# Layer-1 experts of a fused two-layer kernel: the 176 inner rows as 128 and 48 instead of 88 and 88

## The chip, the core and the metric

The kernel runs on one core of one Trainium2 chip. The metric is the device time of one execution in microseconds (us). Before the change the median of three runs is 1293.78 us (1292.96 to 1298.01). One further execution was recorded by the hardware profiler; all views quoted here come from it.

## The reference, cut to what matters

Two transformer layers on x of shape 2 x 1024 x 128 in fp32. The change lies in the second layer's mixture of experts. There are 2048 tokens, 16 experts, and each token goes to four of them:

```python
g = jnp.einsum('th,eih->tei', x, gate_proj)      # gate_proj, up_proj: 16 x 176 x 128
u = jnp.einsum('th,eih->tei', x, up_proj)
act = jax.nn.silu(g) * u
y = jnp.einsum('tei,ehi,te->th', act, down_proj, combine_w)   # down_proj: 16 x 128 x 176
```

`combine_w` is zero except for the four experts a token has chosen. So 8192 pairs of token and expert have to go through a 128 -> 176 -> 128 gated product.

## The kernel before

**Slots and blocks.** The tokens are sorted by expert. Each expert gets a whole number of blocks of 128 slots; at most 79 blocks are needed (`NBLK`), and 79 are always computed. `sort1` computes on VectorE the slot of every choice (`slot_of`, L861) and the weight row of every block (`weight_row`). `scatter` (L898, GpSimd) writes token rows of 512 bytes to `slots_x` in DRAM; `gather` (L910) later reads rows of 512 bytes from `slots_y` in DRAM, multiplied by their share and added to the residual on GpSimd.

**Weights.** `regroup` (L884 to L890) copies, early in the kernel, the weights of every expert into one DRAM table `wx`: for each expert 128 rows of `WX` = 608 floats (2432 bytes), namely 176 gate columns, 176 up columns and two lots of 128 down columns. The inner 176 rows are handled as two halves of 88 (`I1H`), so only 88 of the 128 rows of the down part are used and the other 40 are filled with zeros.

**The stage of the experts.** It is one stretch of the second layer's attention: the loop at the end of the kernel writes the order of TensorE by hand, and at step `EXPERTS` = 67 of 129 it calls `experts()`, which issues all 79 blocks with no attention work between them. All other engines get their order from the scheduler; each engine, and the queue of SP that issues nearly all DMAs, runs its instructions strictly in that order.

For each block i:

- `fetch_w(i)` (SP, L948) brings the 128 x 608 weights of the block's expert into a ring of 6 places. Four places are the tiles that held the normalised tokens and their transposes; two are in the tiles `p` of the attention ("room" in the trace). Blocks 0 to 3 are fetched before the stage, at step `EXPERTS - 2`.
- `fetch_x(g)` (SP, L959) brings four blocks of tokens; `turn_x(g)` transposes them (TensorE L974, ScalarE L976).
- `hidden(i)`: four products on TensorE with weights of 128 rows x 88 columns (L984), sigmoid on ScalarE (L987), two multiplications on VectorE (L988, L989), each on 88 partitions x 256.
- `outputs(i)`, two blocks later: two products with a contraction of 88 (L999) accumulate into one 128 x 128 result. Every four blocks ScalarE copies the results (L1002) and SP stores them to `slots_y` (L1003).

The slots of a group of four blocks lie in DRAM as "(i p) d": row 128 i + p of the group is partition p of block i, so a transfer of a group moves pieces of 512 bytes.

**Tiles that the change shares.** `by_position` writes its result `rel` (L1139, L1141) in the pool `early`, of which there is one buffer, and sends it to DRAM (`bounce`, L1148); `near_by` reads it back skewed (`near`, L1159). Steps 65 and 70 call them for the group of queries that the attention scans next.

An fp32 product counts as two MATMUL instructions in the trace (a transposition as one), so a block has 8 of L984 and 4 of L999.

Of the kernel before, what the change touches and what calls it, by code (L numbers as in the profile page):

```python
# [10 lines left out]
F32 = mybir.dt.float32  # L11
# [7 lines left out]
P = 128  # L19
D = 128  # L20
# [13 lines left out]
E1, I1, K1, G1, KG1 = 16, 176, 4, 4, 2  # L34
M0 = E0 * I0 // P
SH1 = 2 * I1
I1H = I1 // 2
WX = 4 * I1H + 2 * D

NBLK = (B * T * K1 + E1 * (P - 1)) // P  # L40
NTT = B * NT
# [8 lines left out]
def fused_layers_kernel(ctx: ExitStack, tc: tile.TileContext, a: dict, out: bass.AP):  # L50
# [348 lines left out]
                nc.scalar.copy(yT, y)  # L399


    slots_x = dram.tile([NBLK * P, D], F32, tag="slots_x", name="slots_x")
    wx = dram.tile([E1 * P, WX], F32, tag="wx", name="wx")
    slots_y = dram.tile([NBLK * P, D], F32, tag="slots_y", name="slots_y")

# [416 lines left out]
    def sort1():  # L822

        wide = [P, NTT, E1]
        some = l1w.tile(wide, F32, tag="some", name="some")
        at = l1w.tile(wide, F32, tag="at", name="at1")
        count = l1w.tile([P, 4, E1], F32, tag="count", name="count")
        n_tok, n_blk, start_, end_ = (count[:, i, :] for i in range(4))
        slot = l1w.tile([P, NTT, K1], F32, tag="slot", name="slot")
        flat = [t.rearrange("p t e -> p (t e)") for t in (some, at)]  # L830
        nc.vector.tensor_add(some, chosen[0], chosen[1])
        nc.vector.tensor_add(some, some, chosen[2])
        yield
# [12 lines left out]
        nc.vector.tensor_add(at[:, 1:, :], at[:, 1:, :], some[:, 0:NTT - 1, :])  # L846
        by_e = [P, E1, E1]
        nc.vector.tensor_tensor(some, spread(n_tok, NTT), filled.unsqueeze(1).to_broadcast(by_e), ALU.is_gt)
        nc.vector.tensor_reduce(n_blk, some, AX.X, ALU.add)
        yield  # L850
        nc.vector.tensor_tensor(some, lower, n_blk.unsqueeze(1).to_broadcast(by_e), ALU.mult)
        nc.vector.tensor_reduce(start_, some, AX.X, ALU.add)
        nc.vector.tensor_add(end_, start_, n_blk)
        nc.vector.tensor_scalar(start_, start_, float(P), None, ALU.mult)
        yield
        nc.vector.tensor_tensor(at, at, start_.unsqueeze(1).to_broadcast(wide), ALU.add)
        for j in range(K1):
            nc.vector.tensor_mul(some, chosen[j], at)
            nc.vector.tensor_reduce(slot[:, :, j], some, AX.X, ALU.add)
            yield  # L860
        nc.vector.tensor_copy(slot_of, slot)  # L861
        row = l1w.tile([P, NBLK], F32, tag="row", name="row")
        for lo in range(0, NBLK, NTT):
            n = min(NTT, NBLK - lo)
            nos = block_no[:, lo:lo + n]
            nc.vector.tensor_tensor(some[:, 0:n, :], end_.unsqueeze(1).to_broadcast([P, n, E1]),
                                    spread(nos, E1), ALU.is_le)
            nc.vector.tensor_reduce(row[:, lo:lo + n], some[:, 0:n, :], AX.X, ALU.add)
            yield
        nc.vector.tensor_scalar(row, row, float(E1 - 1), float(P), ALU.min, ALU.mult)  # L870
        nc.vector.tensor_copy(weight_row, row[0:1, :])

    def clear(i):

        n = min(4, NBLK - 4 * i)
        nc.sync.dma_start(slots_x[4 * i * P:(4 * i + n) * P, :].rearrange("(i p) d -> p i d", p=P),
                          zeros.unsqueeze(1).to_broadcast([P, n, D]))

    def regroup(i):


        by_row = wx.rearrange("(e p) w -> p e w", p=P)
        if i < 2:
            nc.sync.dma_start(by_row[:, :, i * I1:(i + 1) * I1],  # L884
                              a[("gproj", "uproj")[i]].rearrange("p (e w) -> p e w", e=E1))
        else:
            c = slice(2 * I1 + (i - 2) * D, 2 * I1 + (i - 1) * D)
            nc.sync.dma_start(wx.rearrange("(e p) w -> e p w", p=P)[:, 0:I1H, c],
                              a["dproj"].rearrange("(e j p) d -> j e p d", j=2, p=I1H)[i - 2])
            nc.sync.dma_start(by_row[I1H:P, :, c], zeros[I1H:P].unsqueeze(1).to_broadcast([P - I1H, E1, D]))  # L890

    scatters, fetched = [], {}

# [36 lines left out]

    held = {}
    block_w, block_x, block_xT, block_h, block_y, first_row = {}, {}, {}, {}, {}, {}

    def fetch_w(i):
        if i >= NBLK:
            return
        if i % 6 < 4:
            t = const.tile([P, T], F32, tag=("xn10", "xn11", "xT10", "xT11")[i % 6], name="blockw")
        else:
            t = held["p"][i % 2][:, 0:T]  # L940
# [7 lines left out]
        nc.sync.dma_start(t[:, 0:WX], wx[bass.ds(first_row.pop(i), P), :])  # L948
        block_w[i] = t

    def fetch_x(g):
        if 4 * g >= NBLK:
            return
        n = min(4, NBLK - 4 * g)
# [4 lines left out]
        d = nc.sync.dma_start(  # L959
            t[:, 0:n, :], slots_x[4 * g * P:(4 * g + n) * P, :].rearrange("(i p) d -> p i d", p=P)  # L960
        )
# [5 lines left out]
    def turn_x(g):  # L967
        if 4 * g >= NBLK:
            return
        n = min(4, NBLK - 4 * g)  # L970
        ps = quads(small())
        x = block_x.pop(g)
        for i in range(n):
            nc.tensor.transpose(ps[:, i, :], x[:, i, :], ident)  # L974
        t = quads(held["p"][1][:, T + TB * (g % 2):T + TB * (g % 2 + 1)])
        nc.scalar.copy(t[:, 0:n, :], ps[:, 0:n, :])  # L976
        block_xT[g] = t

    def hidden(i):

        w, xT = block_w[i], block_xT[i // 4][:, i % 4, :]
        ps = quads(small())[0:I1H]
        for j in range(4):
            nc.tensor.matmul(ps[:, j, :], w[:, j * I1H:(j + 1) * I1H], xT, start=True, stop=True)  # L984
        sg = w[0:I1H, WX:WX + 2 * P].rearrange("p (i c) -> p i c", c=P)
        h = pools["late"].tile([P, 2, P], F32, tag="bh", name="bh", bufs=3)[0:I1H]
        nc.scalar.activation(sg, ps[:, 0:2, :], AF.Sigmoid)  # L987
        nc.vector.tensor_mul(sg, ps[:, 0:2, :], sg)  # L988
        nc.vector.tensor_mul(h, ps[:, 2:4, :], sg)  # L989
        block_h[i] = h  # L990

    def outputs(i):
        g, n = i // 4, min(4, NBLK - i // 4 * 4)
        if i % 4 == 0:
            block_y[g] = quads(small())
        ps, h, w = block_y[g], block_h.pop(i), block_w.pop(i)
        for j in range(2):
            c = 4 * I1H + j * D
            nc.tensor.matmul(ps[:, i % 4, :], h[:, j, :], w[0:I1H, c:c + D], start=(j == 0), stop=(j == 1))  # L999
        if i % 4 == n - 1:  # L1000
            t = quads(pools["late"].tile([P, TB], F32, tag="yu", name="by"))
            nc.scalar.copy(t[:, 0:n, :], ps[:, 0:n, :])  # L1002
            nc.sync.dma_start(  # L1003
                slots_y[4 * g * P:(4 * g + n) * P, :].rearrange("(i p) d -> p i d", p=P), t[:, 0:n, :]
            )

    def experts():

        held["p"] = [pools["late"].tile([P, NG * TB], F32, tag="p", name="room", bufs=2) for _ in range(2)]
        turn_x(0)  # L1010
        for i in range(4, 6):
            fetch_w(i)
        for i in range(NBLK + 2):
            if i < NBLK:
                hidden(i)
            if i >= 2:
                outputs(i - 2)
                fetch_w(i + 4)
            if i % 4 == 1:
                turn_x(i // 4 + 1)  # L1020
                fetch_x(i // 4 + 2)

    yT1 = {}

# [582 lines left out]
```

## Time and profile before

| what | value |
|---|---|
| median of three runs | 1293.78 us |
| the profiled execution | 1295.13 us, of which 1293.0 us from first to last instruction |
| mean granted TensorE clock | 0.956 |
| TensorE matmul busy | 1161.0 us, 90% |
| VectorE, ScalarE, GpSimd busy | 782.9, 613.0, 370.4 us |
| DMA | 204.77 MB, mean 158 GB/s |
| the stage of the experts, from its first product to the first product of the attention behind it | 868.77 to 995.17 us |

The page cuts the span in 40 slices of 32.3 us; the stage fills the end of the 27th, the next three and most of the 31st:

```profile
PE   5989899989989777897999999988999999998997
PEclk8999999998999867899999999999999999998998
DMA  6955843445233331363356645579996454563511
```

Each digit is a share in tenths. In the stage both TensorE and the DMA engines are at 9, and nowhere else are the DMA engines that busy for so long.

Transfers of the stage, as the page lists them (size, count):

```profile
blockw<-wx SPq DMA_DIRECT2D x53, 304.0 KB
room<-wx SPq DMA_DIRECT2D x26, 304.0 KB
```

To read the other views: a line of a timeline has the start, the time to the last end, engine, line of the code, operation, output and inputs, shape and count; on TensorE "128\*88" stands for weights of 128 rows and 88 columns. PE are the products, PEld the loads of their weights. "[3.77 <-DMA room<-wx]" is idle time before the line and what ended it. In the chain of waits each line is the work, wait or transfer that the end of the kernel depended on at that time.

### The profile page before, as it was taken

What the parts mean: (1) busy time and instruction counts of PE and PEld (TensorE: products, weight loads), DVE (VectorE), ACT (ScalarE), POOL (GpSimd) and SP (SyncE); (2) the same over time, 40 slices, a digit from 0 to 9 for tenths busy, and PEclk for the clock granted to TensorE, in tenths of its full rate; (3) what the DMA queues carried; (4) which work ended last, traced back from release to release, by engine and by line L of the source; (5) the groups of instructions that cost most, each with busy time, mean ns of one, the idle gap of its engine ahead of it and who ended that gap; (6) DMA issues with size and microseconds to landing.
All of it is one profiled execution on the core that took longest, in us unless ns stands there. A gap on an engine that the chain in (4) does not pass through costs nothing.

```text
span 1293.0 us, 24010 instructions
## 1 busy us (share of the span) xinstructions
PE 1161.0 (90%) x8781; PEld 577.1 (45%) x8781; DVE 782.9 (61%) x2420; ACT 613.0 (47%) x1102; POOL 370.4 (29%) x475
## 2 busy tenths in 40 slices
PE   5989899989989777897999999988999999998997
PEld 2233232354533233443444344458998444443434
DVE  7565654376434756877866756764555766665653
ACT  3644444545655211453555645453444545554463
POOL 1223155310044610001003444320000445445454
PEclk8999999998999867899999999999999999998998
DMA  6955843445233331363356645579996454563511
GB/s 186 238 152 156 259 126 110 133 128 149 85 93 122 111 106 49 98 196 99 125 170 211 208 138 169 188 229 281 288 287 201 138 185 158 174 216 120 174 50 29
DMA packets 196313, 204.77 MB, mean 158 GB/s; under 512 B 26436, under 2 KB 178244, under 8 KB 196196
## 3 DMA queue, kind: packets, MB, share of 16 engines
q1 hardware_dynamic: 189892, 190.12, 47.7%
q0 software_dynamic: 6304, 13.12, 3.4%
q8 instruction: 70, 1.15, 0.4%
q14 instruction: 47, 0.39, 0.1%
HBM read 121.29 MB, written 90.42 MB: 164 GB/s over the span
## 4 chain that ended last, share of the span: by engine, by line
PE 63%; DVE 19%; DMA 8%; issue 5%; ACT 3%; POOL 2%; SPq 0%; POOLq 0%; DVEq 0%; ACTq 0%
PE sm L1245 11%; PE sm L1184 8%; PE acc L1264 8%; PE sm L1235 5%; PE big L731 4%; PE acc L758 4%; PE sm L984 4%; DVE maxima L1209 3%; PE big L362 3%; DVE junk L1204 3%; PE sm L1135 3%; PE big L363 2%; DMA got<-slots_y,slot_of 2%; PE ffn L391 2%; DMA room<-wx 2%
## 5 line engine op out<-in xcount | busy, mean ns | idle before, releaser
L1252 ACT ACTIVATE p<-sm 128x512 f32<-128x512 f32 x512 | 264.8, 605 | 231.3 <-PE sm L1245 224.2
L1209 DVE TENSOR_REDUCE maxima<-sm 128x1 f32<-128x512 f32 (+3 forms) x472 | 226.8, 502 | 101.6 <-PE sm L1184 101.6
L737 ACT ACTIVATE at<-big 128x1024 f32<-128x1024 f32 (+1 forms) x192 | 144.9, 809 | 139.4 <-PE big L731 134.1
L1204 DVE CUSTOM_DVE_ANT_0 junk<-sm,near 128x384 f32<-128x384 f32 (+2 forms) x292 | 130.3, 446 | 64.3 <-PE sm L1184 63.9
L1264 PE MATMUL acc<-p,vs 128*32 128x512 f32 (+1 forms) x1288 | 145.2, 520 | 0.4 <-issue 0.4
L1235 PE MATMUL sm<-ident,near 128*128 128x128 f32 x704 | 109.8, 290 | 25.9 <-DVE maxima L1204 11.2
L731 PE MATMUL big<-qm,xT 32*128 32x512 f32 (+3 forms) x768 | 109.5, 556 | 7.6 <-DVE qm L724 3.8
L1235 PEld LDWEIGHTS sm<-ident,near 128*128 128x128 f32 x704 | 79.7, 145 | 80.5 <-ACT p L1252 35.4
L1245 PE MATMUL sm<-qa,kls 32*128 32x512 f32 (+3 forms) x832 | 112.3, 556 | 0.0
L1184 PE MATMUL sm<-kls,qs 32*128 32x512 f32 (+2 forms) x776 | 105.8, 572 | 6.7 <-POOL kls L1116 5.4
L910 POOL DMA_INDIRECT got<-slots_y,slot_of x64 | 64.9, 1014 | 163.1 <-ACT p L1252 152.6
L758 PE MATMUL acc<-at,xn 128*32 128x512 f32 (+3 forms) x768 | 86.8, 526 | 8.3 <-DVE attn L343 5.3
L743 POOL TENSOR_SCALAR_AFFINE_SELECT at<-at 128x512 f32<-128x512 f32 x64 | 41.8, 654 | 179.8 <-ACT at L737 175.9
L898 POOL DMA_INDIRECT slots_x<-xn,slot_of x64 | 62.4, 976 | 94.6 <-ACT p L1252 84.8
L1139 ACT COPY rel<-sm 128x512 f32<-128x512 f32 x112 | 57.5, 599 | 61.5 <-PE sm L1135 61.5
L920 POOL TENSOR_SCALAR got<-got,share 128x128 f32<-128x128 f32 x64 | 41.4, 646 | 113.4 <-DMA got<-slots_y,slot_of 113.0
L1264 PEld LDWEIGHTS acc<-p,vs 128*32 128x32 f32 x1288 | 26.5, 108 | 103.7 <-issue 94.8
L1184 PEld LDWEIGHTS sm<-kls,qs 32*128 32x128 f32 x776 | 36.5, 186 | 80.8 <-ACT p L1252 21.1
L731 PEld LDWEIGHTS big<-qm,xT 32*128 32x128 f32 x768 | 40.6, 190 | 66.3 <-issue 41.2
L1135 PE MATMUL sm<-posd,qs 32*128 32x256 f32 x448 | 58.1, 422 | 11.9 <-DVE maxima L1209 10.9
L1116 POOL TENSOR_SCALAR khs<-kf,not_aux,k_add 128x1024 f32<-128x1024 f32 x8 | 9.6, 1195 | 187.7 <-PE sm L1245 187.7
L1245 PE MATMUL sm<-qa,khs 32*128 32x512 f32 (+3 forms) x512 | 60.9, 509 | 0.0
(333 smaller groups left out, 1742.8 us busy)
## 6 DMA issues: line engine op xcount, KB each, us to landing
bounce<-rel SPq DMA_DIRECT2D x64, 768.0 KB
near<-bounce SPq DMA_DIRECT2D x64, 768.0 KB
blockw<-wx SPq DMA_DIRECT2D x53, 304.0 KB
slots_y<-by SPq DMA_DIRECT2D x35, 256.0 KB
cb<-cw SPq DMA_DIRECT2D x64, 128.0 KB
bw<-wx SPq DMA_DIRECT2D x64, 128.0 KB
room<-wx SPq DMA_DIRECT2D x26, 304.0 KB
slots_x<-zeros SPq DMA_DIRECT2D x19, 256.0 KB
```

The lines of the kernel that those rows point to most:

```text
L731: nc.tensor.matmul(halves[r // 2][:, r % 2, off:TB], xT0[b][g, kt * P:(kt + 1) * P], masked[b, s][g, q * TB + off:(q + 1) * TB], start=Tru ...
L737: e = nc.scalar.activation(at[:, 2 * j:2 * j + 2, off:TB], sc[:, :, off:TB], AF.Sigmoid, scale=4.0 / math.sqrt(HD))
L758: nc.tensor.matmul(y[32 * r:32 * r + 32, off:TB], xn0[b][:, kt * P + 32 * r:kt * P + 32 * r + 32], at[:, r, off:TB], start=(kt == 0), stop ...
L910: d = nc.gpsimd.indirect_dma_start(y, None, slots_y[:, :], bass.IndirectOffsetOnAxis(ap=slot_of[:, t, j:j + 1], axis=0))
L1135: nc.tensor.matmul(ps[r][:, j, :], qs[g, t:t + P], posd[g, :], start=True, stop=True)
L1184: nc.tensor.matmul(ps[r][:, (k0 - lo) * P:(k1 - lo) * P], qs[g, qt * P:(qt + 1) * P], (kh if far else kl)[g, k0 * P:k1 * P], start=True, s ...
L1204: nc.vector.tensor_tensor_reduce(junk[:, 0:(k1 - k0) * P], part, near[n, i][:, r, w0:w0 + (k1 - k0) * P], 1.0, -BIG, ALU.add, ALU.max, mx[ ...
L1209: nc.vector.tensor_reduce(mx[:, r, slot:slot + 1], part, AX.X, ALU.max)
L1235: nc.tensor.matmul(ps[r][:, i * P:(i + 1) * P], near[n, i][:, r, w0:w0 + P], ident, is_transpose=True, start=(i == close[0]), stop=False, ...
L1245: nc.tensor.matmul(ps[r][:, i0 * P:i1 * P], k[g, kt * P:(kt + 1) * P], qa[n][g, i0 * P:i1 * P], start=(m == 0 and not close), stop=(m == l ...
L1252: e = nc.scalar.activation(p[:, r, :], ps[r], AF.Exp)
L1264: nc.tensor.matmul(y[rows_of(r), part], vs[:, kt, rows_of(r)], probs[n, kt][:, r, part], start=(kt == 0), stop=(kt == NT - 1 and part.stop ...
```

## The change

The inner 176 rows of an expert are split into 128 and 48. A block now has three products for gate and up: 128 gate columns, 128 up columns, and one of 112 columns that holds the last 48 gate columns in its output rows 0 to 47, 16 columns that nobody uses, and the last 48 up columns in output rows 64 to 111. The down part has a product with a contraction of 128 and one with a contraction of 48, whose operands lie on partitions 64 to 111. Two blocks share one sigmoid and two multiplications of each part. The order of TensorE is: hidden part of pair j, outputs of pair j - 2.

The weights of a block are 128 rows x 496 floats (1984 bytes), in a ring of 12 places, two to a tile, and 48 rows x 128 floats from a second table `wd`, by a DMA of their own into the tile `rel` of the attention, which is held for the length of the stage. Of these 12 places 8 are now fetched at step `EXPERTS - 1`. Slots of a group lie as "(p i) d", so a group's transfer moves pieces of 2 KB; six small VectorE operations in place of one turn a slot's number into its row.

```diff
-I1H = I1 // 2
-WX = 4 * I1H + 2 * D
+I1R = I1 - P
+IU = I1 + I0
+WX = IU + P + D
...
-        nc.vector.tensor_copy(slot_of, slot)
...
+        nc.vector.tensor_copy(s0, slot)
+        nc.vector.tensor_scalar(lo, s0, P - 1, 2, ALU.bitwise_and, ALU.logical_shift_left)
+        nc.vector.tensor_scalar(hi, s0, 7, 3, ALU.logical_shift_right, ALU.bitwise_and)
+        nc.vector.tensor_scalar(s0, s0, 9, 9, ALU.logical_shift_right, ALU.logical_shift_left)
+        nc.vector.tensor_tensor(lo, lo, hi, ALU.bitwise_or)
+        nc.vector.tensor_tensor(slot_of, s0, lo, ALU.bitwise_or)
+        yield
...
+    def of_four(slots, g):
+        return slots[4 * g * P:4 * (g + 1) * P, :].rearrange("(p i) d -> p i d", p=P)
...
+        if i == 0:
+            nc.sync.dma_start(by_row[:, :, 0:I1], gate)
+        elif i == 1:
+            nc.sync.dma_start(by_row[:, :, I1:IU], up[:, :, I1 - I0:])
+            nc.sync.dma_start(by_row[:, :, IU:IU + P], up[:, :, 0:P])
+        elif i == 2:
+            nc.sync.dma_start(wx.rearrange("(e p) w -> e p w", p=P)[:, :, IU + P:], down[:, 0:P, :])
         else:
...
+            nc.sync.dma_start(wd.rearrange("(e p) d -> e p d", p=P)[:, 0:I1R, :], down[:, P:, :])
...
+        if i == 0:
+            held["rel"] = early.tile([P, 2 * NG * NEAR], F32, tag="rel", name="room")
...
-        nc.sync.dma_start(t[:, 0:WX], wx[bass.ds(first_row.pop(i), P), :])
-        block_w[i] = t
+        row = first_row.pop(i)
+        nc.sync.dma_start(t, wx[bass.ds(row, P), :])
+        rest = held["rel"][I0:I0 + I1R, k * P:(k + 1) * P]
+        nc.sync.dma_start(rest, wd[bass.ds(row, I1R), :])
+        block_w[i] = t, rest
...
+        for k in range(n):
+            i = 2 * j + k
+            w, xT = block_w[i][0], block_xT[i // 4][:, i % 4, :]
+            for m in range(2):
+                nc.tensor.matmul(ps[:, 2 * m + k, :], w[:, m * IU:m * IU + P], xT, start=True, stop=True)
+            nc.tensor.matmul(ps2[0:I0 + I1R, k, :], w[:, P:IU], xT, start=True, stop=True)
...
+        nc.scalar.activation(h, ps[:, 0:n, :], AF.Sigmoid)
+        nc.scalar.activation(h2[g2], ps2[g2], AF.Sigmoid)
+        nc.vector.tensor_mul(h, ps[:, 0:n, :], h)
+        nc.vector.tensor_mul(h, ps[:, 2:2 + n, :], h)
+        nc.vector.tensor_mul(h2[u2], ps2[g2], h2[g2])
+        nc.vector.tensor_mul(h2[u2], ps2[u2], h2[u2])
...
+            nc.tensor.matmul(ps, h[:, k, :], w[:, IU + P:], start=True, stop=False)
+            nc.tensor.matmul(ps, h2[:, k, :], rest, start=False, stop=True)
...
-        for i in range(NBLK + 2):
-            if i < NBLK:
-                hidden(i)
-            if i >= 2:
-                outputs(i - 2)
-                fetch_w(i + 4)
-            if i % 4 == 1:
-                turn_x(i // 4 + 1)
-                fetch_x(i // 4 + 2)
+        for j in range(N_PAIRS + 2):
+            if j < N_PAIRS:
+                hidden(j)
+            if j >= 2:
+                outputs(j - 2)
+                for k in range(2):
+                    fetch_w(2 * (j - 2) + RING + k)
+            if j % 2 == 0:
+                turn_x(j // 2 + 1)
+                fetch_x(j // 2 + 3)
...
-    for i in range(4):
-        beside(EXPERTS - 2, fetch_w, i)
+    for i in range(8):
+        beside(EXPERTS - 1, fetch_w, i)
```

More of the change, by code (lines that the diff above doesn't have):

```diff
@@ L399, in close_unit @@
                 nc.scalar.copy(yT, y)
-    slots_x = dram.tile([NBLK * P, D], F32, tag="slots_x", name="slots_x")
+    slots_x = dram.tile([-(-NBLK // 4) * 4 * P, D], F32, tag="slots_x", name="slots_x")
     wx = dram.tile([E1 * P, WX], F32, tag="wx", name="wx")
-    slots_y = dram.tile([NBLK * P, D], F32, tag="slots_y", name="slots_y")
+    wd = dram.tile([E1 * P, D], F32, tag="wd", name="wd")
+    slots_y = dram.tile([-(-NBLK // 4) * 4 * P, D], F32, tag="slots_y", name="slots_y")
     wx0 = dram.tile([E0 * P, 3 * P], F32, tag="wx0", name="wx0")
@@ L860, in sort1 @@
             yield
-        nc.vector.tensor_copy(slot_of, slot)
+        s0, lo, hi = (t.bitcast(U32)[:, 0:NTT * K1].rearrange("p (t k) -> p t k", k=K1)
+                      for t in (flat[0], flat[1], chosen[0].rearrange("p t e -> p (t e)")))
+        nc.vector.tensor_copy(s0, slot)
[5 more added lines that the diff above has]
+        yield
         row = l1w.tile([P, NBLK], F32, tag="row", name="row")
@@ L871, in sort1 @@
         nc.vector.tensor_copy(weight_row, row[0:1, :])
+    def of_four(slots, g):
+        return slots[4 * g * P:4 * (g + 1) * P, :].rearrange("(p i) d -> p i d", p=P)
     def clear(i):
-        n = min(4, NBLK - 4 * i)
-        nc.sync.dma_start(slots_x[4 * i * P:(4 * i + n) * P, :].rearrange("(i p) d -> p i d", p=P),
-                          zeros.unsqueeze(1).to_broadcast([P, n, D]))
+        nc.sync.dma_start(of_four(slots_x, i), zeros.unsqueeze(1).to_broadcast([P, 4, D]))
+        n = NBLK - 4 * i
+        if n < 4:
+            nc.sync.dma_start(of_four(slots_y, i)[:, n:, :], zeros.unsqueeze(1).to_broadcast([P, 4 - n, D]))
     def regroup(i):
         by_row = wx.rearrange("(e p) w -> p e w", p=P)
-        if i < 2:
-            nc.sync.dma_start(by_row[:, :, i * I1:(i + 1) * I1],
-                              a[("gproj", "uproj")[i]].rearrange("p (e w) -> p e w", e=E1))
-        else:
[L887 to L890, printed above, removed]
+        down = a["dproj"].rearrange("(e i) d -> e i d", i=I1)
+        gate, up = (a[n].rearrange("p (e w) -> p e w", e=E1) for n in ("gproj", "uproj"))
+        if i == 0:
[5 more added lines that the diff above has]
+            nc.sync.dma_start(wx.rearrange("(e p) w -> e p w", p=P)[:, :, IU + P:], down[:, 0:P, :])
+        else:
+            nc.sync.dma_start(wd.rearrange("(e p) d -> e p d", p=P)[:, 0:I1R, :], down[:, P:, :])
     scatters, fetched = [], {}
@@ L932, in fused_layers_kernel @@
     block_w, block_x, block_xT, block_h, block_y, first_row = {}, {}, {}, {}, {}, {}
+    RING = 12
+    N_PAIRS = -(-NBLK // 2)
     def fetch_w(i):
@@ L936, in fetch_w @@
             return
-        if i % 6 < 4:
-            t = const.tile([P, T], F32, tag=("xn10", "xn11", "xT10", "xT11")[i % 6], name="blockw")
-        else:
-            t = held["p"][i % 2][:, 0:T]
+        if i == 0:
+            held["rel"] = early.tile([P, 2 * NG * NEAR], F32, tag="rel", name="room")
+        k = i % RING
+        if k < 8:
+            if k % 2 == 0:
+                held[k // 2] = const.tile([P, T], F32, tag=("xn10", "xn11", "xT10", "xT11")[k // 2], name="blockw")
+            t = held[k // 2]
+        else:
+            t = held["p"][k // 2 % 2]
+        t = t[:, k % 2 * WX:(k % 2 + 1) * WX]
         if i % 4 == 0:
@@ L953, in fetch_x @@
             return
-        n = min(4, NBLK - 4 * g)
         if g < 2:
@@ L958, in fetch_x @@
             t = quads(held["p"][0][:, T + TB * (g % 2):T + TB * (g % 2 + 1)])
-        d = nc.sync.dma_start(
-            t[:, 0:n, :], slots_x[4 * g * P:(4 * g + n) * P, :].rearrange("(i p) d -> p i d", p=P)
-        )
+        d = nc.sync.dma_start(t, of_four(slots_x, g))
         for name in scatters:
@@ L969, in turn_x @@
             return
-        n = min(4, NBLK - 4 * g)
         ps = quads(small())
         x = block_x.pop(g)
-        for i in range(n):
+        for i in range(4):
             nc.tensor.transpose(ps[:, i, :], x[:, i, :], ident)
         t = quads(held["p"][1][:, T + TB * (g % 2):T + TB * (g % 2 + 1)])
-        nc.scalar.copy(t[:, 0:n, :], ps[:, 0:n, :])
+        nc.scalar.copy(t, ps)
         block_xT[g] = t
[L979 to L1000, printed above, removed]
+    def hidden(j):
+        n = min(2, NBLK - 2 * j)
+        ps, ps2 = quads(small()), quads(small())[:, 0:n, :]
+        for k in range(n):
[4 more added lines that the diff above has]
+            nc.tensor.matmul(ps2[0:I0 + I1R, k, :], w[:, P:IU], xT, start=True, stop=True)
+        h = pools["late"].tile([P, 2, P], F32, tag="bh", name="bh", bufs=3)[:, 0:n, :]
+        c = RING * P + 2 * P * (j % 4)
+        h2 = held["rel"][:, c:c + 2 * P].rearrange("p (k c) -> p k c", c=P)[:, 0:n, :]
+        g2, u2 = slice(0, I1R), slice(I0, I0 + I1R)
+        nc.scalar.activation(h, ps[:, 0:n, :], AF.Sigmoid)
[4 more added lines that the diff above has]
+        nc.vector.tensor_mul(h2[u2], ps2[u2], h2[u2])
+        block_h[j] = h, h2[u2]
@@ new lines, in outputs @@
+    def outputs(j):
+        h, h2 = block_h.pop(j)
+        for k in range(min(2, NBLK - 2 * j)):
+            i = 2 * j + k
+            g = i // 4
+            if i % 4 == 0:
+                block_y[g] = quads(small())
+            ps, (w, rest) = block_y[g][:, i % 4, :], block_w.pop(i)
+            nc.tensor.matmul(ps, h[:, k, :], w[:, IU + P:], start=True, stop=False)
+            nc.tensor.matmul(ps, h2[:, k, :], rest, start=False, stop=True)
+        if i % 4 == 3 or i == NBLK - 1:
+            n = i % 4 + 1
@@ L1001, in outputs @@
             t = quads(pools["late"].tile([P, TB], F32, tag="yu", name="by"))
[L1002 to L1005, printed above, removed]
+            nc.scalar.copy(t[:, 0:n, :], block_y[g][:, 0:n, :])
+            nc.sync.dma_start(of_four(slots_y, g)[:, 0:n, :], t[:, 0:n, :])
     def experts():
@@ L1010, in experts @@
         turn_x(0)
-        for i in range(4, 6):
+        fetch_x(2)
+        for i in range(8, RING):
             fetch_w(i)
-        for i in range(NBLK + 2):
-            if i < NBLK:
-                hidden(i)
-            if i >= 2:
-                outputs(i - 2)
-                fetch_w(i + 4)
-            if i % 4 == 1:
-                turn_x(i // 4 + 1)
-                fetch_x(i // 4 + 2)
+        for j in range(N_PAIRS + 2):
[8 more added lines that the diff above has]
+                fetch_x(j // 2 + 3)
     yT1 = {}
```

## The prediction

> **What bounds the kernel now.** I read the page's slices first (TensorE and DMA both at 9 in the stage of the experts), then busy time by stage, the chain of waits, and TensorE's and SP's timelines there. Nothing outside the stage is on the path of this change, so the sum is made for the stage, 868.77 to 995.17 us.
>
> Busy time by stage (us, then busy us and count of TensorE, weight loads, VectorE, ScalarE, GpSimd; granted clock, DMA share, GB/s):
>
> ```profile
> 868.77:995.17 126.40, 118.21 (x1025) 114.83 (x1026) 66.28 (x159) 51.69 (x118) 0.00 (x0) 0.99 0.91 275
> 900.00:980.00 80.00, 76.64 (x676) 74.29 (x675) 43.53 (x105) 33.73 (x78) 0.00 (x0) 1.00 0.95 289
> ```
>
> TensorE is busy 96% and the DMA engines 95%: two limits almost level. VectorE (half) and ScalarE (0.4) are not the bound. Which of the two is ahead is read from TensorE's timeline, in a part without waits:
>
> ```profile
> 882.59 1.04 PE L984 MATMUL sm<-room,blockw 128*88 128x128 f32 x8
> 883.46 0.61 PE L999 MATMUL sm<-room,bh 88*128 88x128 f32 x4
> 883.91 1.04 PE L984 MATMUL sm<-room,blockw 128*88 128x128 f32 x8
> ...
> 887.42 0.61 PE L999 MATMUL sm<-blockw,bh 88*128 88x128 f32 x4
> 887.87 0.60 PE L974 MATMUL sm<-ident,room 128*128 128x128 f32 x4
> ```
>
> Start to start, a block is 883.91 - 882.59 = 1.32 us: 0.87 for four products of L984 (0.22 each) and 0.45 for two of L999. Four transpositions are 0.44. Four blocks are 4 x 1.32 + 0.44 = 5.72 us, 79 blocks 19.75 x 5.72 = 113.0 us. The stage takes 126.4, so 13.4 us are waits and a slow clock. In the chain of waits the transfers of weights stand in between every five or so blocks; they ring with six places. The largest wait is at the start:
>
> ```profile
> 873.43 0.61 PE L999 MATMUL sm<-blockw,bh 88*128 88x128 f32 x4
> 877.81 1.55 PE L984 MATMUL sm<-room 128*88 128x128 f32 x8 [3.77 <-DMA room<-wx]
> ```
>
> Four blocks were fetched ahead and are used up at 874. The fifth comes at 877.8, behind the `near` transfers (SP's timeline):
>
> ```profile
> 858.32 1.42 SPq L948 DMA_DIRECT2D blockw<-wx  x3
> 859.79 0.97 SPq L959 DMA_DIRECT2D bx<-slots_x  x2
> 863.42 0.91 SPq L1148 DMA_DIRECT2D bounce<-rel  x2
> 868.49 2.60 SPq L1159 DMA_DIRECT2D near<-bounce  x2
> 871.68 0.90 SPq L948 DMA_DIRECT2D room<-wx  x2
> ```
>
> **TensorE, what goes.** One product of four for gate and up: 0.22 per block, 0.88 per four blocks. The remaining ones have 128 or 112 columns in place of 88; L999, with 128, has 0.45/4 = 0.112 per instruction against L984's 0.87/8 = 0.109: 24 x 0.003 = +0.06.
>
> **TensorE, what comes.** The built program gives the product with a contraction of 48 a tile of 64 rows x 128 columns at row 64; before, all of the stage has the full 128 x 128. So in each block TensorE goes from full to half array and back: full (L1038), half (L1039), 158 changes in all. [...] No 64-row tile occurs in the trace; the nearest row is L395, one product with a contraction of 32 between full-array products (twice; here once):
>
> ```profile
> 402.74 1.13 PE L391 MATMUL ffn<-h,sw 128*128 128x512 f32 x2
> 403.79 1.12 PE L395 MATMUL ffn<-cwT,b 32*128 32x512 f32 x2
> 404.84 0.66 PE L1029 MATMUL big<-ident,yT 128*128 128x128 f32 x4
> ```
>
> Both last 1.05 us from start to next start. Two such instructions with no change of mode are closer:
>
> ```profile
> 160.82 1.02 PE L363 MATMUL big<-xT,w 128*128 128x512 f32 x2
> ```
>
> Its second one (592 ns) starts 1.02 - 0.59 = 0.43 after the first, so a pair is 0.86. [...] Bounds: 0, if 48 rows ran like 88 (88 shows no loss), and 0.20. [...] A return onto transpositions is 0.05 cheaper. Per four blocks: 8 x 0.19 - 0.05 = +1.47.
>
> Sum: 5.72 - 0.88 + 0.06 + 1.47 = 6.37 per four blocks, x 19.75 = **125.8 us**, against 113.0. The halved number of sigmoids and multiplications doesn't shorten TensorE; per pair VectorE still has four (4 x 0.42 = 1.7 us of 3.2), ScalarE 2 x 0.38 + 0.6; both stay hidden.
>
> **DMA.** Per block before: 304 KB weights, 64 KB tokens, 64 KB results, 442 kB; after: 248 + 24 + 128 KB = 410 kB. At the 289 GB/s of the stage that is 1.42 us, below TensorE's new 1.59, without any gain from the 2 KB pieces. So DMA stops being the bound and the ring of 12 (six pairs) hides its latency: of the 13.4 us of waits, the ones inside the stage go. SP issues 10 DMAs per four blocks at 0.45 (0.90 for two above): 4.5 us of 6.4, hidden.
>
> **The start.** The order of SP in the built program decides it. Block 0's weights go out early as now (775 us), but block 0's 48 rows need the tile `rel`, which is free only when the `bounce` writes of step 65 have landed. The scheduler therefore puts these rows, and all of blocks 1 to 7, behind `near<-bounce`; before, blocks 1 to 3 went at 858.32. The hidden part of the first pair needs block 1. It goes where `room<-wx` goes now, at 871.7, behind 1.5 MB of `near`, and lands as that did: TensorE starts at 877.8 in place of 868.77. Blocks 2 and 3 follow at about 0.9 us each, as fast as the first pairs use them. The clock is also lost in this wait; now, after 3.8 us of idling, the row is:
>
> ```profile
> 877.80:882.00 4.20, 4.19 (x23) 4.20 (x24) 0.84 (x2) 0.48 (x2) 0.00 (x0) 0.59 0.75 235
> ```
>
> 0.41 of 4.2 us, 1.7 us, and after nine idle the same or a little more. The wait itself has no cover: TensorE has nothing else queued.
>
> **End of stage:** 877.8 + 1.7 + 125.8 = 1005.3, less 0.3 for the transpositions of the first group (done before) = 1005.0. No wait at the end: the last block's results now follow 3 us after its hidden part. Against 995.2 that is **+9.8 us**. Behind the stage attention goes on bound by TensorE, and its `near` tiles are loaded, so the delay goes to the end in full.
>
> **Elsewhere, counted as nothing.** Six VectorE operations of 64 elements for one (196 ns, at 617.7): some 1 us in a part where VectorE is 61% busy; `slot_of` is not read until 693.5. Regrouping at 148 to 206 us: the up rows go in pieces of 256 and 512 bytes, one more DMA, but two fills with zeros go; the transfers have until 775 to land, and the `cb` loads queued behind them are far from late. If that cover failed it were 1 to 2 us.
>
> The sum stands against the profiled execution's 1295.13 us, 1.35 above the median: 1304.9 there, **1303.6** for the median.
>
> **Rivals.**
>
> 1. *The change of mode is free* (48 rows run like 88, or beside the next). For: 88-row and 96-row products show no loss. Against: every pair of modes in this trace shows it. TensorE is then 4.90 per four blocks and DMA the bound: 79 x 1.42 = 112 us, from 876 when `near` is through, less the two groups of tokens fetched before, plus about 1 for the last outputs: 987, **8 us faster, 1286**; with a gain from 2 KB pieces, down to 1275. It decides below 0.12 us per change, where the sign turns.
> [...]
> 3. *Supply still late.* There are twice the DMAs of weights per block, and the built program keeps eight in flight by its semaphores, so 3.2 blocks. A weights transfer takes 4.7 us under load (the chain's DMA pieces); 4.7/3.2 = 1.47 is below 1.59. From 5.1 us on it would bind; at 6 us it is 1.88 per block, 148 us: **1325**. Against: DMA load falls.
> 4. *The early fetch works*, i.e. blocks 1 to 7 come before the stage: 868.8 + 125.5, about **1293**. Against: the order is fixed in the program; SP can't pass a waiting instruction.
>
> **Chances.** Forecast 0.68 (own range 1299 to 1309), rival 1 0.14, rival 2 with 4 0.09, rival 3 0.09. The range 1291 to 1312 leaves out most of rival 1 and rival 3. Half a per cent is about what this kernel's measurement tells from no change. Slower is the forecast and rival 3 (0.77) less 0.03 for a forecast that lands under 1300; faster 0.15, same 0.11, slower 0.74.
>
> **What would show it.** Right: L1038 and L1039 starting 0.2 apart at each change, a pair of blocks at about 3.2 us; TensorE idle from 868 to 877.8 until DMA `blockw<-wx`; DMA share of the stage near 0.85; stage end near 1005. Wrong: pairs at 2.5 us with DMA at 0.95 (rival 1), waits for `room<-wd` or weights in the middle of the stage (rival 3), or a first product before 872 (rival 4).

## The result, and the profile after

| | before | after |
|---|---|---|
| median | 1295.31 us (4 runs) | 1311.18 us (4 runs: 1304.32, 1311.52, 1310.84, 1315.61) |
| ratio | | 1.0104, 95% interval 1.0073 to 1.0135 |
| profiled execution | 1295.13 us | 1304.32 us |
| the stage, from the last attention product ahead of it to the first behind it | 128.15 us | 137.77 us |

The change made the kernel slower, by the stage of the experts and by something besides: the stage accounts for 9.6 us, the medians differ by 15.9.

Busy time by stage in the profile after: the stage from its first product, and its middle (columns as before).

```profile
871.65:1007.51 135.86, 128.78 (x866) 109.50 (x867) 67.31 (x161) 47.41 (x119) 0.00 (x0) 0.96 0.80 245
900.00:980.00 80.00, 80.00 (x554) 67.93 (x552) 42.39 (x101) 29.43 (x76) 0.00 (x0) 1.00 0.84 253
```

In the middle TensorE is busy 80.00 of 80 us while the DMA engines fell from 0.95 to 0.84: the bound moved to TensorE alone, although it runs fewer instructions (554 in place of 676). TensorE's timeline there shows what fills it, the outputs of two blocks:

```profile
930.88 0.39 PE L1038 MATMUL sm<-blockw,bh 128*128 128x128 f32 x2
931.20 0.48 PE L1039 MATMUL sm<-room 48*128 48x128 f32 x2
931.62 0.49 PE L1038 MATMUL sm<-blockw,bh 128*128 128x128 f32 x2
932.03 0.48 PE L1039 MATMUL sm<-room 48*128 48x128 f32 x2
932.45 0.66 PE L1002 MATMUL sm<-ident,room 128*128 128x128 f32 x4
```

From the second line on, it is 0.41 to 0.42 from the start of a product of two instructions to the next start, where 2 x 0.11 = 0.22 would do: 0.19 to 0.20 for a switch between the full array and the 48 rows. (The first line shows only 0.10 of its switch; the sum over a pair of blocks, below, gives 0.19 per switch.)

The start of the stage, first on SP's queue, then on TensorE:

```profile
866.29 0.92 SPq L1189 DMA_DIRECT2D bounce<-rel  x2
870.96 3.57 SPq L1200 DMA_DIRECT2D near<-bounce  x2
874.72 0.36 SPq L980 DMA_DIRECT2D room<-wd  x1
875.26 0.36 SPq L978 DMA_DIRECT2D blockw<-wx  x1
```

```profile
872.20 0.38 PE L1017 MATMUL sm<-room,blockw 128*112 128x128 f32 x2
879.66 1.22 PE L1016 MATMUL sm<-room,blockw 128*128 128x128 f32 x4 [7.08 <-DMA blockw<-wx]
```

Block 1's weights leave SP at 875.26, behind `bounce` and `near`, and TensorE stands idle for 7.08 us. Then it runs at half clock for five us (clock 0.50, third figure from the right):

```profile
879.60:884.60 5.00, 4.94 (x23) 4.94 (x24) 1.69 (x4) 1.61 (x4) 0.00 (x0) 0.50 0.93 291
```

### The profile page after: what moved, and what is told of

The parts are those of the page before. It is cut to its first block, busy times and chain, and to the rows that moved or that the text cites. A ratio compares the mean times of both kernels' runs of the same rounds, so it can differ in the third digit from the quotient of the medians.

```text
span 1302.6 us, 23878 instructions
## 1 busy us (share of the span) xinstructions
PE 1166.1 (90%) x8624; PEld 568.4 (44%) x8624; DVE 788.0 (60%) x2427; ACT 609.0 (47%) x1103; POOL 369.1 (28%) x475
## 4 chain that ended last, share of the span: by engine, by line
PE 47%; DVE 10%; DMA 3%; ACT 2%; issue 2%; POOL 1%; SPq 0%; DVEq 0%; ACTq 0%
PE sm L1286 10%; PE sm L1225 8%; PE acc L1305 8%; PE sm L1276 6%; PE sm L1016 3%; DVE maxima L1250 3%; PE sm L1176 3%; DVE junk L1245 3%; PE sm L1039 3%; PE sm L1038 2%; DMA got<-slots_y,slot_of 2%; PE sm L1017 1%; ACT p L1293 1%; PE sm L1002 1%; PE sm L1260 1%
```

## Where the rest came from: the two traces laid side by side

The products outside the stage are the same in both kernels, so each one's start after, less its start before, gives a curve of delays. It is flat except at a few places. The table has the steps (us) of the profiles that bear on the argument, against the first profile of before; "stage" is its length less 128.15.

| profile | at 184 us | at 625 | at 775 | at 858 | stage |
|---|---|---|---|---|---|
| after | 3.68 | 2.71 | 1.45 | 1.59 | 9.62 |
| again (same kernel) | 3.68 | 2.70 | 1.49 | 1.60 | 9.61 |
| e1_order | 3.68 | 2.71 | 1.48 | 1.60 | 0.27 |
| e2_full | 3.68 | 2.71 | 1.47 | 1.60 | -1.08 |
| e3_early | 3.67 | 2.71 | 1.49 | 1.59 | 8.83 |
| m2_512 | 2.09 | -0.01 | 0.00 | 1.59 | 9.57 |
| e3n_start | 2.09 | 2.71 | 1.49 | 1.59 | 5.26 |
| h1_regroup | 0.00 | 2.72 | 1.47 | 1.60 | 9.53 |
| sp1_queue | 3.74 | 2.72 | 1.47 | 1.59 | 1.49 |
| before_again | 0.00 | 0.00 | 0.01 | 0.00 | 0.81 |
| m1_price (before's code up to the stage) | 0.00 | 0.00 | 1.58 | 1.62 | 22.06 |

The first two steps are in neither before_again nor m1_price, whose code ahead of the stage is that of before, so they belong to the change: 3.7 + 2.7 = 6.4 us. The last two, 3.0 us, need no changed code: m1_price has both, and its code up to the stage is the old one. The changed versions pay them in nearly every profile; whether the change makes them more frequent is not shown.

With 9.6 for the stage the four steps make 19.1 us; behind the stage the delay shrinks again by 2.9 (after) and 2.5 us (again). That leaves 16.2 to 16.6, close to the 15.9 between the medians. The agreement is rough: smaller steps come and go from profile to profile, also in before's code (-1.9 us ahead of 176 us in m1_price). In the profile of after they are -3.5 us ahead of 176 us and -3.5 between 204 and 600, so this execution was only 9.2 us slower than the profiled one of before.

**At 184 us** TensorE waits for VectorE, in layer 0 (timelines of after, VectorE and TensorE):

```profile
182.37 0.75 DVE L377 SCALAR_TENSOR_TENSOR t<-big,b,sg 128x512 f32<-128x512 f32 x1 [3.07 <-ACT sg L376]
183.16 0.75 DVE L378 SCALAR_TENSOR_TENSOR h<-big,b,t 128x512 f32<-128x512 f32 x1
183.82 1.89 DVE L380 TENSOR_TENSOR h<-h,cb 128x512 f32<-128x512 f32 x3
```

```profile
184.56 1.20 PE L392 MATMUL ffn<-h,w 128*128 128x512 f32 x2 [2.17 <-DVE h L380]
```

Three multiplications by `cb` stand together ("x3"); before, each followed its own unit. TensorE has been idle since 182.4. The line itself was not touched by the change: the scheduler put these instructions in another order. The step is 2.1 us of waiting and 1.6 of half clock behind it; m2_512 and e3n_start have the same wait of 2.17 us and no half clock, and their step is 2.09.

**At 625 us** the six operations that turn slot numbers into rows (the last is L872) stand on VectorE, which works without a gap here, in front of the maxima. VectorE and TensorE in after, then the same wait in before:

```profile
616.05 0.22 DVE L872 TENSOR_TENSOR slot_of<-some,at 128x64 uint32<-128x64 uint32 x1
621.18 2.46 DVE L1250 TENSOR_REDUCE maxima<-sm 128x1 f32<-128x512 f32 x4
621.91 0.44 PE L1276 MATMUL sm<-ident,near 128*128 128x128 f32 x2 [1.86 <-DVE maxima L1250]
```

```profile
623.99 0.44 PE L1235 MATMUL sm<-ident,near 128*128 128x128 f32 x2 [0.72 <-DVE maxima L1209]
```

In after the clock behind it is 0.61:

```profile
621.60:625.20 3.60, 3.29 (x26) 1.60 (x26) 2.05 (x4) 0.84 (x2) 0.00 (x0) 0.61 0.39 138
```

**At 775 and 858 us** the idle time is the one of before (2.44 us), but the clock behind it falls to a half in the changed kernel. In m1_price it does so in old code (its wait at 775, and the clock from 772.20 to 775.60):

```profile
772.00 0.78 PE L1236 MATMUL sm<-ident,near 128*128 128x128 f32 x3 [2.45 <-DVE maxima L1210]
```

```profile
772.20:775.60 3.40, 3.40 (x19) 0.89 (x17) 2.20 (x4) 0.72 (x2) 0.17 (x1) 0.50 0.31 109
```

What decides is where the wait lies. In each of the traces the granted clock changes only at whole multiples of 3.41 us from its first change (38 stretches of constant clock in before, 38 in after). In all eleven profiles whose wait at 775 us lies within one such step, but for at most 0.25 us, the half clock follows; in before, before_again and m2_512 a step's edge divides the wait (1.65 and 0.79 us in before), and it does not. So a delay of a few us anywhere ahead can bring this half clock or take it away.

## The experiments

All ratios are to the kernel before, measured beside it. "Stage" as in the first table; "pace" is the time for four blocks, from the fourth to the twentieth group of transpositions.

| run | median us | ratio (95%) | stage us | pace us |
|---|---|---|---|---|
| before (profile) | | | 128.15 | 6.15 |
| again | 1310.39 | 1.0105 (1.0069 to 1.0141) | 137.8 | 6.38 |
| e1_order | 1304.04 | 1.0057 (1.0039 to 1.0074) | 128.4 | 5.94 |
| e2_full | 1303.12 | 1.0057 (1.0037 to 1.0076) | 127.1 | 5.99 |
| e3_early | 1312.56 | 1.0096 (1.0063 to 1.0129) | 137.0 | 6.39 |
| m1_price | 1317.22 | 1.0177 (1.0134 to 1.0220) | 150.2 | 7.17 |
| m2_512 | 1306.93 | 1.0079 (1.0046 to 1.0112) | 137.7 | 6.39 |
| e3n_start | 1306.58 | 1.0080 (1.0050 to 1.0110) | 133.4 | 6.38 |
| before_again | 1295.71 (one) | | 129.0 | 6.22 |
| h1_regroup | 1308.25 | 1.0093 (1.0066 to 1.0119) | 137.7 | 6.38 |
| sp1_queue | 1303.19 | 1.0046 (1.0020 to 1.0072) | 129.6 | 6.14 |
| c1_all | 1292.73 | 0.9968 (0.9950 to 0.9985) | 119.4 | 5.71 |
| c2_buffers | 1287.15 | 0.9954 (0.9936 to 0.9973) | 116.9 | 5.54 |

### The changed kernel again

> The changed kernel once more, unaltered, in five rounds. Forecast (the price of the tile-mode changes and the late start): the ratio to the kernel before stays near 1.010, the stage of experts again lasts about 136 us from its due start to its end (TensorE's first full run of products near 879.7, end near 1007.6 in the profile), and no stage outside it differs by more than a chance 2 us. If the slowdown were an accident of the first runs (the profiled 1304 against the other three near 1311), the ratio falls below 1.005.

The ratio repeats. The stage is the same to 0.1 us. The four steps outside it repeat too (table above); this expectation still took all differences there for chance.

### Half of the mode changes

```diff
+            two = (h[:, k, :], w[:, IU + P:]), (h2[:, k, :], rest)
+            for m, (x, y) in enumerate(two[::-1] if k else two):
+                nc.tensor.matmul(ps, x, y, start=(m == 0), stop=(m == 1))
```

> The second block of each pair takes its 48-row product first and its 128-row product after it, so that the two 48-row products of a pair stand side by side: 4 tile-mode changes per four blocks in place of 8; all products, transfers and waits are the same. Forecast theory (a change costs 0.19 us of TensorE): TensorE's work per four blocks falls from 6.37 by 4 x 0.18 = 0.7 to about 5.65 us, which is where DMA binds (410 kB x 4 at 289 GB/s = 5.68), so a stage pace of 5.7 to 6.0 in place of 6.48 and a time 9 to 15 us below the changed kernel. Rival (the 48-row products, their transfers or the longer chain through the vector engines cost the time, not the change of mode): the pace stays at 6.4 to 6.5 and the time within 3 us of the changed kernel.

TensorE's timeline now has the two 48-row products of a pair in one line:

```profile
907.55 0.39 PE L1040 MATMUL sm<-blockw,bh 128*128 128x128 f32 x2
907.87 0.71 PE L1040 MATMUL sm<-room 48*128 48x128 f32 x4
908.50 0.49 PE L1040 MATMUL sm<-blockw,bh 128*128 128x128 f32 x2
```

From 907.55 to 908.83 (the next line's start) the four products take 1.28 us, against 1.57. The stage fell by 9.3 us to the length of before. The time fell by 6.4 us, less than the 9 to 15 expected. The pace of 5.94 is within the 5.7 to 6.0 expected, but above TensorE's 5.65.

### No mode change

```diff
+            nc.gpsimd.memset(held["rel"][0:I0, 0:RING * P + 8 * P], 0.0)
...
-        block_w[i] = t, rest
+        block_w[i] = t, held["rel"][0:I0 + I1R, k * P:(k + 1) * P]
...
-        block_h[j] = h, h2[u2]
+        block_h[j] = h, h2[0:I0 + I1R]
```

The sigmoid's scratch moves to spare columns, so that the rows of zeros stay zero.

> The 48-row product becomes a product over 112 rows, of which the first 64 are zeros (written once), so that it uses the whole array: no tile-mode change at all; the same count of products, the same columns, the same transfers. Forecast theory: TensorE's work per four blocks falls by 8 x 0.18 = 1.4 to about 4.95 us, DMA binds at 5.5 to 5.9 per four, and the time is 11 to 18 us below the changed kernel, only 0 to 4 us below the version with half of the changes. If a change costs half of what is forecast, this one is 7 us below and the version with half of the changes 3.5. Rival (the small product itself costs it): within 3 us of the changed kernel, TensorE's work per four still above 6.

A product over 112 rows, 64 of them zeros, costs the plain 0.22:

```profile
906.97 0.39 PE L1041 MATMUL sm<-blockw,bh 128*128 128x128 f32 x2
907.20 0.39 PE L1042 MATMUL sm<-room 112*128 112x128 f32 x2
907.42 0.39 PE L1041 MATMUL sm<-blockw,bh 128*128 128x128 f32 x2
```

TensorE is busy 70.49 of the 80 us from 900 to 980 where the changed kernel has 80.00. But the time fell by 7.3 us, not by the 11 to 18 expected: pace and time are those of half the changes, and something else holds both near 5.95. DMA share is 0.88 in both, not the 0.95 of before, so SP's queue comes next (below).

### The price by itself, in the kernel before

```diff
-            nc.tensor.matmul(ps[:, i % 4, :], h[:, j, :], w[0:I1H, c:c + D], start=(j == 0), stop=(j == 1))
+            r = slice(0, 48 if j else I1H)
+            nc.tensor.matmul(ps[:, i % 4, :], h[r, j, :], w[r, c:c + D], start=(j == 0), stop=(j == 1))
```

> The kernel before, in which the second output product of each block takes only the first 48 of its 88 rows (40 rows of inner sums per block are left out), so that it changes the array's tile mode twice per block, as the changed kernel does, with none of the change's transfers, layouts or queues. Forecast theory (0.18 to 0.19 us per change): TensorE's work per four blocks rises from 5.72 by 8 x 0.18 = 1.45 to about 7.2 us, TensorE becomes what binds the stage, its pace goes from 6.13 to 7.2 per four, and the time rises by about 20 us over the kernel before (1313 to 1317); half the price gives 6.45 per four and +6 us; a free change gives 6.1 per four and no difference.

Only one product takes fewer rows (40 rows of inner sums are left out of its result), nothing else was touched, and the kernel became 1.8% slower. TensorE's timeline (compare 0.45 between these two lines in the prediction's fence):

```profile
932.77 0.80 PE L1000 MATMUL sm<-room,bh 88*128 88x128 f32 x4
933.50 1.11 PE L984 MATMUL sm<-room,blockw 128*88 128x128 f32 x8
```

Four blocks take 7.13 us in place of 5.72: 1.41 / 8 = 0.18 per change. With e1_order, where the order alone was changed, and e2_full, where only zeros were added, that settles what the time is paid for, the change between the full array and the 48 rows, and its price.

### Earlier weights

The first eight `blockw<-wx` are issued ahead of all `room<-wd`; `fetch_rest` holds the two lines for `rest` of `fetch_w`.

```diff
     for i in range(8):
-        beside(EXPERTS - 1, fetch_w, i)
+        beside(EXPERTS - 1, fetch_w, i, True)
+    for i in range(8):
+        beside(EXPERTS - 1, fetch_rest, i)
```

> The 128-row weights of blocks 0 to 7 are issued before any transfer of 48 rows, so that blocks 0 and 1 stand ahead of the last bounce and near transfers on SP's queue; nothing else is changed. Forecast theory (late start costs 8 to 9 us of the stage): TensorE's first full run of gate and up products begins near 871 in place of 879.7, the pace stays TensorE's (6.4 per four), and the time is 6 to 10 us below the changed kernel. Rival (the early start is given back, because the transfers set the pace or another transfer is late instead): the first products begin early but the stage ends within 3 us of the changed kernel's end, with new waits for DMA in its middle.

The rival won: the first products came early, and the stage became only 0.8 us shorter; the time did not fall. TensorE's timeline:

```profile
886.79 0.46 PE L1046 MATMUL sm<-room 48*128 48x128 f32 x2 [3.31 <-DMA room<-wd]
...
889.51 1.12 PE L1009 MATMUL sm<-ident,room 128*128 128x128 f32 x4 [1.43 <-DMA room<-slots_x]
```

The idle time moved to the next things in the queue, and the half clock came behind it as before. So the `near` transfers were taken off SP's queue:

```diff
+                if f is positions and t == EXPERTS - 2:
+                    by_position(*args)
+                    beside(EXPERTS, near_by, *args, nc.gpsimd)
```

> As the version with the early weights, and the two near transfers that stood ahead of the 48-row weights on SP's queue are issued on GpSimd's queue behind the experts' first transfers instead. Theory now (in the version before, the idle only moved: TensorE waited 3.3 us for the 48 rows and 1.4 us for tokens, both queued behind these two, and the clock fell to 0.74 once more): no idle over 2 us remains at the start of the stage, which then lasts 126 to 130 us in place of 137.8, and the time is 6 to 11 us below the changed kernel. Rival (the supply of weights cannot keep up with an earlier start): new waits for weights in the first 30 us, and the stage lasts 134 us or more.

The stage fell by 4.4 us of the 8 to 12 expected. SP's timeline shows what still stands in front:

```profile
871.40 0.92 SPq L1196 DMA_DIRECT2D bounce<-rel  x2
878.05 3.92 SPq L987 DMA_DIRECT2D room<-wd  x8
882.61 0.36 SPq L997 DMA_DIRECT2D room<-slots_x  x1
```

The 48 rows go into `rel`, so they wait for `bounce` to land, 6.7 us later, and the tokens stand behind them: TensorE waits 2.92 us for `room<-slots_x` at 886.86. By this reading the rest of the late start is the price of using `rel`; no run put the 48 rows elsewhere.

### Old slot rows, a second profile of before, an earlier layout

```diff
-        s0, lo, hi = (t.bitcast(U32)[:, 0:NTT * K1].rearrange("p (t k) -> p t k", k=K1)
...
+        nc.vector.tensor_copy(slot_of, slot)
...
-        return slots[4 * g * P:4 * (g + 1) * P, :].rearrange("(p i) d -> p i d", p=P)
+        return slots[4 * g * P:4 * (g + 1) * P, :].rearrange("(i p) d -> p i d", p=P)
```

> The changed kernel with the slots in the old order (rows of 512 bytes instead of 2 KB), so that the slot numbers need no reordering: the five operations that reorder them on VectorE go as well. Theory now: inside the stage TensorE binds, so its length stays at 136 to 139 us; outside it, TensorE's wait for the maxima at about 625 us falls back from 1.83 to 0.72 us, and the 3 us of half clock behind it go, together 2 to 3 us less than the changed kernel. Rival (the 2 KB rows carry the stage): the stage is 3 us longer or more.

In the stage nothing changed (137.7 us), so the 2 KB pieces carry nothing while TensorE binds. The wait at 625 us is back to

```profile
626.50 0.44 PE L1269 MATMUL sm<-ident,near 128*128 128x128 f32 x2 [0.64 <-DVE maxima L1243]
```

and the clock behind it to 1.00. The step at 775 went as well, which I had not expected, and one of 1.4 us with half clock came at 829. The idle time at 775 is as long in m2_512 as in the changed kernel, but the clock behind it is another. Windows of 3.6 us from the end of that idle time, first in the changed kernel, then in m2_512:

```profile
772.80:776.40 3.60, 3.58 (x19) 1.22 (x19) 2.42 (x4) 0.58 (x2) 0.39 (x2) 0.56 0.42 150
```

```profile
775.70:779.30 3.60, 3.56 (x37) 1.56 (x39) 2.44 (x4) 1.87 (x4) 0.41 (x2) 1.00 0.33 118
```

> The kernel before once more, for a second profile. If the change itself makes the two half-clock stretches behind the idle at about 775 and 857 us, they are absent here too, and the clock lost between 600 us and the stage is near 2.7 us; if they come and go by chance, this profile can show one or both, and 4 to 8 us lost. The waits at 184 us (for the product with cb) and at 625 us (0.72 us for the maxima) stay as in the first profile.

None of the four steps: see the table. This does not make the two at 775 and 858 us the change's: the waits of this profile lie as in the first one (1.64 and 0.80 us on the two sides of an edge at 775), and m1_price, where they lie otherwise, has both.

```diff
-        at(62 + 4 * i, regroup, i)
+        at(44 + 4 * i, regroup, i)
```

> The changed kernel with the four calls that lay out the experts' weights in memory 18 places earlier in layer 0 (their transfers are the same). With that the order of VectorE's instructions in layer 0 is again that of the kernel before: each product with cb follows its own unit, where the changed kernel puts three of them behind the third unit. Theory: TensorE's wait of 2.16 us at 184 us goes, and 1.5 us of half clock behind it, so 3 to 4 us less than the changed kernel (ratio to the kernel before 1.007 to 1.008), the stage of experts unchanged at 137 to 139 us. Rival (the wait comes from the transfers themselves, which keep cb from landing): the wait stays near 2 us there or moves to where these transfers run now.

The step at 184 us is gone, 0.00 in the trace, and VectorE's order is the old one (VectorE, and TensorE without a wait):

```profile
183.47 0.69 DVE L380 TENSOR_TENSOR h<-h,cb 128x512 f32<-128x512 f32 x1
186.46 1.12 PE L392 MATMUL ffn<-h,w 128*128 128x512 f32 x2
```

The ratio fell only from 1.0105 to 1.0093, where 1.007 to 1.008 was expected; the intervals overlap, so the trace shows this gain and the medians don't. It is the new layout's calls at their old place in the program that displaced those instructions. Why the scheduler decides so was not tried.

### SP's queue, and all repairs together

To the version without mode changes:

```diff
-        d = nc.sync.dma_start(t, of_four(slots_x, g))
+        d = (nc.scalar if g > 1 else nc.sync).dma_start(t, of_four(slots_x, g))
...
-            nc.sync.dma_start(of_four(slots_y, g)[:, 0:n, :], t[:, 0:n, :])
+            nc.scalar.dma_start(of_four(slots_y, g)[:, 0:n, :], t[:, 0:n, :])
```

> The version whose 48-row product uses the whole array, with the token loads from the third quad on and all stores of outputs issued by ScalarE instead of SP: 8 issues per four blocks on SP instead of 10. In the two versions with fewer tile-mode changes SP issued without a gap, about 0.54 us apart and 0.4 for a load of addresses, 5.9 us per four, and both ran at 5.92 to 5.93 per four whatever TensorE's work was (5.65 and 4.95). Theory (SP's issues bind there): the pace falls to 5.4 to 5.7 per four, where the bytes bind (1.64 MB per four at 290 to 300 GB/s), and the time is 4 to 9 us below the version without mode changes. Rival (the bytes or the transfers' engines bind already at 5.9): the pace stays within 0.1 of 5.93.

The theory fell: the pace did not improve (6.14, against 5.99 in e2_full), although SP now has gaps. The time is that of e2_full. Its stage also began with a longer wait, 8.08 us where e2_full had 6.42, but the pace is taken behind that.

To that, the early weights, `near` on GpSimd's queue and the earlier layout of the weights, and

```diff
-        for i in range(1 + (t % 4 == 0)):
+        for i in range(1 + (t % 3 == 0)):
             beside(t, route_on)
```

> All repairs at once: no tile-mode change (112 rows), early weights and the near transfers off SP, token loads and stores on ScalarE's queue, the weights' layout 18 places earlier in layer 0, and three more of the routing's steps taken before its last one, so that fewer of VectorE's operations stand in front of the maxima at 625 us. If the parts add up (10.7 us for the mode changes, 4 for the start, 3.7 at 184 us, 4 at 625 and 775, 4 to 7 for SP's queue), it is 23 to 30 us below the changed kernel: 1281 to 1288, faster than the kernel before by 0.5 to 1.1%. If the bytes bind the stage instead, the parts inside it don't add up, and it ends at 1288 to 1296, about level with the kernel before.

1292.73, below before but above the 1281 to 1288 that the sum of parts gave. The stage went to 119.4 us, 3.3 below what two parts give (127.1 - 4.4 = 122.7). Two things did not go: with more of the routing's steps taken earlier, the wait at 625 us only moved ahead (the step from 595 to 632 us is 2.55), and 3.8 us stand right behind the stage, on ScalarE. (e2_full and sp1_queue wait at the same copy already, 3.00 and 4.08 us.)

```profile
989.65 0.58 ACT L1053 COPY by<-sm 128x512 f32<-128x512 f32 x1 [0.62 <-PE sm L1049]
...
993.73 0.48 ACT L1053 COPY by<-sm 128x384 f32<-128x384 f32 x1 [3.49 <-DMA slots_y<-by]
994.73 1.28 ACT L1303 ACT_TABLE_LOAD   x1 [0.52 <-ACT by L1053]
```

The last copy waits for the one buffer, with the attention's exponentials behind it. A second buffer:

```diff
-            t = quads(pools["late"].tile([P, TB], F32, tag="yu", name="by"))
+            t = quads(pools["late"].tile([P, TB], F32, tag=("yu", "x0")[g % 2], name="by"))
```

> The version with all repairs, in which the copies of the outputs of four blocks take two buffers in turn (the second is the one that held the first quad of tokens). In that version ScalarE waited 3.5 us at 990 us for the store of the quad before the last, with the first exponentials of the attention behind it, and TensorE stood 1.3 us and ran at half clock after it (3.7 us later than before the stage's end). If that wait is all of it, the time falls by 2.5 to 4 us, to 1288 to 1291 (ratio 0.993 to 0.995); if the exponentials are held by something else, it stays within 1 us of it.

```profile
985.69 0.48 ACT L1053 COPY by<-sm 128x384 f32<-128x384 f32 x1 [0.81 <-PE sm L1049]
986.69 1.28 ACT L1303 ACT_TABLE_LOAD   x1 [0.52 <-ACT by L1053]
```

The wait is gone, and the pace went from 5.71 to 5.54 as well. The ratio of 0.993 to 0.995 that was expected was a little too good. At 0.9954 (0.9936 to 0.9973) this version is faster than the kernel before, and so than the changed one; against the version ahead of it the intervals overlap.

## Why the prediction held, and where it did not

1303.6 us was forecast, 1311.18 measured, inside 1291 to 1312, though by 0.8 us only; slower was right. The stage was forecast to 0.2 us by the right mechanism. The 6 us that are missing came from elsewhere, and that they fitted into the range is luck.

- **TensorE's work.** 5.72 - 0.88 + 0.06 + 1.47 = 6.37 per four blocks; measured 6.38 to 6.39 in every profile of the changed kernel. The 0.19 per change is a difference of two rows of before, 1.05 us from start to next start at 403.79 (L395, 32 rows) less 0.86 for the pair of L363 without a change; a return onto transpositions adds 0.05 less there: four of them take 0.66 us behind L395 in place of 0.60 (L974), a pair of products 1.12 to 1.13 (L395, L391) in place of 1.02. Taken at 32 rows and 512 columns, the 0.19 held at 48 rows and 128 columns: 0.18 in m1_price, and (1.57 - 0.90 + 0.10) / 4 = 0.19 between after and e2_full (1.57 and 0.90 for the outputs of a pair; 0.10 is the longer first line, L1016 0.71 in place of 0.61, behind the last change). The runs show how long a change takes; what TensorE does in that time no run shows. Rival 1 and half the price fell with m1_price: a free change would have given 6.1 us per four blocks and half the price 6.45, and the pace was 7.17.
- **DMA and rival 3.** In the changed kernel the transfers are hidden: share 0.84, and the start's is the stage's only wait for a transfer. That they would follow at 1.42 us per block once TensorE is fast was too good: e1_order and e2_full stayed near 1.49 (5.94 / 4), and c2_buffers reached 1.39 only with queue, start and buffer mended.
- **The start.** The order on SP was read rightly. The first full run of products came 8.0 us after the stage's first product (9.0 forecast), and the half clock behind it cost 2.5 us (5 us at 0.50), not 1.7. The two errors nearly cancel: 135.9 us from first product to the end, 136.2 forecast. **Rival 4**, an early fetch, was priced as if the weights alone were late. e3_early and e3n_start show that this is worth 0.8 us, and 4.4 with `near` off the queue, not 11.
- **End of stage.** +9.8 forecast, +9.6 in the trace.
- **"Elsewhere, counted as nothing"** is the step that failed. "If that cover failed it were 1 to 2 us" was wrong in size and in kind; it was 6.4 us. The slot operations have nobody waiting for `slot_of`, as I said, but they stand on an in-order engine ahead of the maxima that TensorE does wait for: 1.1 us of idle time, then 1.6 of half clock (shown by m2_512). The regrouping did not hold up `cb` on the queue but the place of its consumers on VectorE: 2.1 us and 1.6 of half clock (shown by h1_regroup). The forecast read the orders of TensorE and SP at the stage, and VectorE's nowhere.
- **What is in no sum.** The 3.0 us at 775 and 858 are half clock behind waits that were always there, and m1_price pays them in old code. Of the three profiles of the old code up to the stage one pays them and two do not, which is too few to say how often. Of the 2.5 to 2.9 us regained behind the stage a part is clock too: between 1170 and 1195 us the first profile of before has half clock for 10.2 us, after for 6.8 and again for 3.4.

What holds the pace near 5.95 in e1_order and e2_full stays open: not TensorE's work (5.65 and 4.95 give the same), nor the number of SP's issues alone (sp1_queue). That the single result buffer is part of it is shown for c1_all to c2_buffers only.

## What to carry to other kernels

A product with a short contraction was not cheaper than a full one here: over 88 and 112 rows it took the 0.22 of one over 128, and where 48 rows alternated with the full array each change cost 0.19 us, almost a whole product. Rows of zeros took that away (e2_full: TensorE busy 70.49 us of 80 in place of 80.00), and the short ones side by side a part of it (e1_order: 1.28 us per pair of blocks in place of 1.57). And when a change adds work to an in-order engine or transfers to a shared queue, look at that engine's order over the whole kernel, not only at the stage that was changed: 6.4 of these sixteen us came from layers and steps the diff barely touches.

## What the runs showed of the hardware

The half clock came behind idle times of 1.86, 2.17 and 2.45 us, and it came in steps of 3.41 us. Whether it came depended on where the wait lay between two such steps: one and the same 2.45 us of idle time is followed by a clock of 0.56 in after and 1.00 in m2_512, and by 0.50 in m1_price where before, with the same code, has 1.00. At 184 and 625 us (idle 2.17 and 1.86) the half clock cost 1.6 us each; at 184 us m2_512 and e3n_start have the same 2.17 without it.
